# Summing the first block of rows of a graph attention layer densely instead of over gathered edges

## The chip, the core and the metric

The kernel runs on one NeuronCore of a Trainium2 chip. Five engines work side by side, each through its own queue in order: TensorE (PE in the profile; its weight loads are shown as PEld), VectorE (DVE), ScalarE (ACT), GpSimd (POOL) and SyncE (SP, which here only issues transfers). The metric is the device time of one launch in microseconds (us); lower is better. One core means one core's span and one granted TensorE clock.

## The reference, cut to what matters

The program is four graph layers in a row over the same 3327 nodes with 512 features, each followed by a residual sum and a layer norm. The adjacency matrix has 26,715 edges in all and its density falls with the row number: the first 128 rows hold 4,829 of them (row 0 has 223 neighbours, row 10 has 62). Only layer 0, a graph attention layer with 8 heads of 64 features, is touched:

```python
Wh = jnp.einsum('nd,hdo->hno', x, W)            # 8 heads x 3327 x 64
f1 = jnp.einsum('hno,ho->hn', Wh, a1)
f2 = jnp.einsum('hno,ho->hn', Wh, a2)
e = jax.nn.leaky_relu(f1[:, :, None] + f2[:, None, :], negative_slope=0.2)
e = jnp.where(adj[None, :, :] > 0, e, NEG_INF)
h_prime = jnp.einsum('hnm,hmo->hno', jax.nn.softmax(e, axis=-1), Wh)
x = _layernorm(x + elu(h_prime as 3327 x 512))
# layer 1: mean over neighbours, two weights, relu; layer 2: mean over the first 64 neighbours;
# layer 3: attention again, 4 heads of 128
```

## The kernel before

The rows are 26 blocks of 128 (the last has 127). For each block the kernel makes an edge list from the adjacency matrix, and each layer then gathers the rows of its neighbours by that list, 128 edges (a chunk) per indirect transfer, and sums them with a selection matrix on TensorE. The lists of block 1 to 25 have 19 down to 5 chunks, 201 together. Block 0 is too dense for one list: three lists (`HEAVY`, L527) of 14 chunks, 42 together.

**Edge lists** (`structure`, L848). Python generators order the work. A block's two halves of the adjacency matrix are loaded into two tiles `ab` (one buffer each, 832 KB, L857), turned into a 0/1 mask by ScalarE (L864), multiplied by a code of the column (L874) and searched on VectorE for the eight largest values of each segment (L892). For block 0 each segment is searched three times, with the found values replaced between (L894). L904 and L906 sort the candidates into slots, and L943 to L957 spread the slots over the 128 partitions as `idx` and `dst`. Each `yield` in `structure` is one turn; a regular block takes five to seven turns, block 0 takes 30 (three lists of ten) and one more at its end. The order of the blocks is 1, 2, 3, 0, 4, ... (`FIRST`, L543). Layers 2 and 3 and the second half of layer 1 treat block 0 by its dense mask `row0` and need no list of it; layer 0 alone uses its three lists.

**Prologue.** While lists are made, `projection` (L1338) loads each block of `x`, transposes it, multiplies it by the weights of layer 0 (L1017) and stores rows of 528 numbers (8 heads of 64 features and two scores) to the table `t0_d`. After each projection three turns of `structure` are taken. `finish` (L1034) closes the table; the first gather can then start.

**Layer 0.** The loop at L1480 takes one group of up to four chunks per step and advances every unfinished generator by one stage (`Stages.step`), and takes one turn of `structure` (two on each eighth step). A group (`Gat.group`, L1188) gathers its chunks on POOL's queue (L981), computes their scores (L1206 to L1231) and weights (L1238), and adds 2 matmuls per chunk into two PSUM tiles `acc` (L1247). The pool of these has four buffers, so that two blocks' sums can be open. After a block's last group `layer0_end` (L1432) divides by the softmax sum (L1260 to L1264), makes elu, residual and layer norm (L1273 to L840), multiplies by the weights of layer 1 (L780) and stores rows to `t1_d`; block 0 to 9 also store a product with a second weight to `z1_d`.

A scheduler decides the order of instructions on each engine up to the end of layer 0 from this program order and its own estimates. From layer 1 on the program order is kept as written. Layer 1 gathers from `t1_d` and so starts when all 26 blocks are stored; four independent products (`self_part`) are placed ahead of it.

Layer 3 already sums its block 0 densely (`first_block`, L1147): for each of the 26 blocks of rows it makes a weight matrix of 128 by 128 per head with VectorE (L1170, L1172), a mask with ScalarE (L1165), and one matmul per head (L1175), with rows that are still in PSUM. This stage is not touched by the change, and its rows serve as prices.

Of the kernel before, what the change touches and what calls it, by code (L numbers as in the profile page):

```python
# [8 lines left out]
F32 = mybir.dt.float32  # L9
# [520 lines left out]
HEAVY = ((0, 9, 1760, 120, 9, 3), (9, 18, 1792, 120, 9, 3), (18, 27, 1792, 120, 9, 3))  # L530
# [12 lines left out]
FIRST = 3  # L543
# [5 lines left out]
class EdgeList:  # L549


    def __init__(self, pool, name, cuts, room, K, rounds, at):
        self.cuts, self.room, self.K, self.rounds, self.at = cuts, room, K, rounds, at
        L = self.L = -(-room // P)
        self.idx = pool.tile([P, L], U32, name=f"idx{name}")
        self.dst = pool.tile([P, L], BF16, name=f"dst{name}")
        self.nmid = pool.tile([P, 1], F32, name=f"nmid{name}")
# [18 lines left out]
class Ring:  # L576
# [20 lines left out]
    def done(self):  # L597

        self.live.pop(0)

# [22 lines left out]
def sparse_path(ctx, tc, flag_i, x, adj, l0_w, l0_a1, l0_a2, l1_w_self, l1_b_self, l1_w_nb, l1_b_nb,  # L623
# [35 lines left out]
    for b in range(NB):  # L659
        parts = HEAVY if b == 0 else ((0, SEGMENTS[b], CAPS[b], SLOTS[b], SEGMENTS[b], 1),)  # L660
        total = parts[-1][1]
        lists.append([])
        for q, (s0, s1, room, K, n, rounds) in enumerate(parts):
            cuts = [int(NP * ((s0 + (s1 - s0) * s / n) / total) ** 2) // 2 * 2 for s in range(n + 1)]
            cuts = [c for i, c in enumerate(cuts) if i in (0, n) or c >= 8 * rounds]
            lists[b].append(EdgeList(keep, f"{b}_{q}", cuts, room, K, rounds, sum(map(len, lists)) - 0))
# [176 lines left out]
    def structure(big, mid, ps, m0):  # L843
# [26 lines left out]
        for k, b in enumerate(order):  # L870
            ab = fetch(order[k + 1]) if k + 1 < NB else None
            val = big.tile([P, NP], U16, name="val")
            for s in range(2):
                nc.vector.tensor_mul(val[:, s * HW:(s + 1) * HW], ms[s], code[:, s * HW:(s + 1) * HW])  # L874
            many = len(lists[b]) > 1
            if many:
                nc.vector.tensor_add(deg[:, b:b + 1], half[:, 0, b:b + 1], half[:, 1, b:b + 1])
                lone = mid.tile([P, 1], F32, name="lone")
                nc.vector.tensor_scalar(lone, deg[:, b:b + 1], 0.0, None, ALU.is_equal)
            for q, l in enumerate(lists[b]):  # L880
                L, K, cuts, rounds, a = l.L, l.K, l.cuts, l.rounds, l.at
                dg = dgs[:, a:a + 1]
                start = starts[:, a:a + 1]
                if not many:
                    nc.vector.tensor_scalar(dg, half[:, 0, b:b + 1], half[:, 1, b:b + 1], 1.0, ALU.add, ALU.max)
                n = (len(cuts) - 1) * rounds
                cand = mid.tile([P, n, 8], F32, name="cand")
                for s in range(len(cuts) - 1):
                    seg = val[:, cuts[s]:cuts[s + 1]]
                    for r in range(rounds):  # L890
                        top = cand[:, s * rounds + r, :]
                        nc.vector.max(out=top, in_=seg)  # L892
                        if r + 1 < rounds:
                            nc.vector.match_replace(out=seg, in_to_replace=top, in_values=seg, imm_value=0.0)  # L894
                    if s == (len(cuts) - 1) // 2:
                        if q == 0 and ab is not None:
# [12 lines left out]
                if not many:  # L909
                    nc.vector.tensor_scalar(slots[:, 0:1], slots[:, 0:1], 1.0, None, ALU.max)  # L910
                elif q == 0:
                    nc.vector.tensor_tensor(slots[:, 0:1], slots[:, 0:1], lone, ALU.max)
                    nc.vector.tensor_tensor(dg, lone, cnt[:, a:a + 1], ALU.max)
                else:
                    nc.vector.tensor_copy(dg, cnt[:, a:a + 1])
# [86 lines left out]
    class Gat:  # L1002
        def __init__(self, name, table, H, OUT, w, k):
# [5 lines left out]
            self.opened, self.free = False, True  # L1009

# [22 lines left out]
        def finish(self, pool, ps):  # L1033
# [5 lines left out]
            n = 4 * H if self.k else 2 * H  # L1039
# [834 lines left out]
```

## Time and profile before

| | us |
|---|---|
| median of 3 runs (lowest, highest) | 1853.08 (1841.69, 1855.64) |
| the profiled execution, its own time | 1863.64 |
| its span | 1861.8 |
| prologue: start to the first group's work | 0 to 224 |
| layer 0 up to the end of block 18 | 224 to 655 |
| of this from block 3's norm to block 0's norm | 349 to 424 |
| last seven blocks of layer 0 up to the first products for layer 1 | 655 to 740 |
| layers 1, 2 and 3 | 740 to 1862 |

The stage boundaries are read from the start of ScalarE's layer norm step (L840) of each block in the trace. The profile gives, per engine, the time that its instructions cover. A matmul's record lasts longer than its place in the stream: the starts of neighbouring records, not their lengths, tell what it costs TensorE. An fp32 matmul stands as two records. A window's answer gives the busy time of each engine in that stretch, the number of instructions, the granted TensorE clock and the mean busy share of the DMA engines. The granted clock of the whole execution was 0.919.

### The profile page before, as it was taken

What the parts mean: (1) busy time and instruction counts of PE and PEld (TensorE: products, weight loads), DVE (VectorE), ACT (ScalarE), POOL (GpSimd) and SP (SyncE); (2) the same over time, 40 slices, a digit from 0 to 9 for tenths busy, and PEclk for the clock granted to TensorE, in tenths of its full rate; (3) what the DMA queues carried; (4) which work ended last, traced back from release to release, by engine and by line L of the source; (5) the groups of instructions that cost most, each with busy time, mean ns of one, the idle gap of its engine ahead of it and who ended that gap; (6) DMA issues with size and microseconds to landing.
All of it is one profiled execution on the core that took longest, in us unless ns stands there. A gap on an engine that the chain in (4) does not pass through costs nothing.

```text
span 1861.8 us, 24835 instructions
## 1 busy us (share of the span) xinstructions
PE 1556.7 (84%) x7669; PEld 1020.7 (55%) x7707; DVE 1232.2 (66%) x3224; ACT 788.8 (42%) x2525; POOL 893.4 (48%) x981
## 2 busy tenths in 40 slices
PE   5898758988989998899999987568997946778774
PEld 4665545665656665455555543135665725666553
DVE  8999857878877863255566765365654525676776
ACT  6557835555666664122111111014443423454564
POOL 1000166556555531655556632666665246666650
PEclk9899879989999999799999989788998977888988
DMA  9524776777675632999999983877887346666661
GB/s 305 206 77 134 263 248 188 261 236 214 235 221 158 214 122 84 385 352 332 320 350 345 376 294 109 274 250 237 282 280 249 130 119 170 187 189 191 199 175 36
DMA packets 126658, 418.72 MB, mean 225 GB/s; under 512 B 23539, under 2 KB 25075, under 8 KB 126516
## 3 DMA queue, kind: packets, MB, share of 16 engines
q0 software_dynamic: 81472, 304.52, 51.4%
q1 hardware_dynamic: 45044, 112.52, 17.1%
q8 instruction: 63, 1.03, 0.2%
q14 instruction: 79, 0.65, 0.1%
HBM read 368.66 MB, written 48.30 MB: 224 GB/s over the span
## 4 chain that ended last, share of the span: by engine, by line
PE 60%; DVE 18%; issue 6%; another core or an unknown queue 6%; ACT 4%; DMA 4%; POOL 1%; SPq 0%; DVEq 0%; ACTq 0%; POOLq 0%
PE po L780 18%; PE acc L1247 18%; PE acc L1555 10%; PE po L1017 5%; DVE cand L892 2%; PE pt L765 2%; PE pg L1218 2%; DMA gm<-t_d,idx 2%; DVE gt L1238 1%; DVE cand L906 1%; PE acc L1175 1%; DVE sl L904 1%; DVE val L874 1%; DVE st L785 1%
## 5 line engine op out<-in xcount | busy, mean ns | idle before, releaser
L981 POOL DMA_INDIRECT gl<-t_d,idx x334 | 331.8, 993 | 273.4 <-issue 73.3
L981 POOL DMA_INDIRECT gt<-t_d,idx x243 | 242.3, 997 | 384.2 <-DVE sl L910 211.2
L1247 PE MATMUL acc<-gt,sel 128*128 128x264 f32 (+2 forms) x972 | 248.7, 403 | 1.3 <-issue 0.7
L1247 PE MATMUL acc<-gl,sel 128*128 128x260 f32 (+3 forms) x684 | 191.6, 430 | 48.1 <-issue 40.1
L981 POOL DMA_INDIRECT gm<-t_d,idx x159 | 159.1, 1001 | 115.3 <-PE acc L1555 55.9
L1247 PEld LDWEIGHTS acc<-gt,sel 128*128 128x128 f32 (+2 forms) x972 | 184.2, 196 | 51.9 <-issue 23.4
L780 PE MATMUL po<-wn,xt 128*128 128x512 f32 x416 | 201.2, 628 | 12.5 <-ACT vc L946 6.1
L1247 PEld LDWEIGHTS acc<-gl,sel 128*128 128x128 f32 (+3 forms) x684 | 139.1, 211 | 82.1 <-issue 51.2
L1238 DVE TENSOR_TENSOR gt<-gt,pg 128x1536 f32<-128x1536 f32 (+3 forms) x75 | 140.6, 1874 | 9.3 <-issue 4.7
L780 PEld LDWEIGHTS po<-wn,xt 128*128 128x128 f32 x416 | 80.8, 200 | 101.6 <-issue 84.4
L1555 PE MATMUL acc<-gm,selr 128*128 128x512 f32 (+2 forms) x360 | 118.6, 460 | 9.0 <-DMA gm<-t_d,idx 5.8
L892 DVE MAX8 cand<-val 128x8 f32<-128x832 uint16 (+38 forms) x259 | 125.1, 522 | 0.0
L1017 PE MATMUL po<-w,xt 128*128 128x262 f32 x416 | 104.0, 406 | 21.4 <-ACT xt L772 21.3
L768 ACT COPY xt<-pt 128x512 f32<-128x512 f32 x81 | 47.4, 591 | 149.2 <-PE pt L765 85.8
L1017 PE MATMUL po<-gt,xt 128*128 128x268 f32 x416 | 108.0, 406 | 2.6 <-ACT xt L772 1.3
L765 PE MATMUL pt<-s_ident,xres 128*128 128x128 f32 x500 | 77.5, 281 | 37.4 <-DMA xres<-in_x_dram 16.5
L1218 PEld LDWEIGHTS <-ds 128*128 128x128 bf16 x1332 | 55.6, 99 | 91.8 <-issue 43.2
L1206 ACT ACTIVATE far<-place,nmid 128x384 int16<-128x384 int16 (+3 forms) x137 | 86.9, 638 | 43.5 <-DVE ds L1210 36.2
L1017 PEld LDWEIGHTS po<-w,xt 128*128 128x128 f32 x416 | 82.2, 201 | 41.6 <-ACT xt L772 24.1
L780 PE MATMUL po<-wx,xt 128*128 128x512 f32 x208 | 97.5, 616 | 4.3 <-ACT vc L946 4.3
L1238 DVE TENSOR_TENSOR gl<-gl,pg 128x1536 f32<-128x1536 f32 (+3 forms) x53 | 98.2, 1852 | 2.2 <-issue 1.2
L1230 ACT ACTIVATE pg<-sc 128x24 f32<-128x24 f32 (+5 forms) x137 | 26.0, 190 | 164.3 <-DVE sc L1229 105.6
(309 smaller groups left out, 3042.4 us busy)
## 6 DMA issues: line engine op xcount, KB each, us to landing
ab<-in_adj_dram SPq DMA_DIRECT2D x25, 832.0 KB
ab<-in_adj_dram SPq DMA_DIRECT2D x25, 831.5 KB
t_d<-t SPq DMA_DIRECT2D x25, 512.0 KB
gm<-t_d POOLq DMA_DIRECT2D x20, 512.0 KB
t_d<-t SPq DMA_DIRECT2D x25, 384.0 KB
t_d<-tg SPq DMA_DIRECT2D x25, 264.0 KB
t_d<-tg SPq DMA_DIRECT2D x25, 260.0 KB
xres<-in_x_dram SPq DMA_DIRECT2D x25, 256.0 KB
```

The source lines that it names most:

```text
L765: nc.tensor.transpose(pt[:, c, :], src[:, c * P:(c + 1) * P], ident)
L768: nc.scalar.copy(xt, pt)
L780: nc.tensor.matmul(po, xt[:, c, :], w[:, c], start=c == 0, stop=c == DC - 1)
L892: nc.vector.max(out=top, in_=seg)
L981: nc.gpsimd.indirect_dma_start(out=t[:m, c, :], out_offset=None, in_=table[:, :], in_offset=bass.IndirectOffsetOnAxis(ap=l.idx[:m, c0 + c: ...
L1017: nc.tensor.matmul(pw[s], xt[:, c, :], self.w[:, c, s, :], start=c == 0, stop=c == DC - 1)
L1206: nc.scalar.activation(far[:, :g * P], place[:, c0 * P:(c0 + g) * P], AF.Abs, bias=l.nmid, scale=2.0)
L1218: nc.tensor.matmul(pe[:, c], ds[:, c * P:(c + 1) * P], self.own[:, k, :, b], start=k == 0, stop=k == 2)
L1230: nc.scalar.activation(w[:, :g], sc[:, :g, 0], AF.Exp)
L1238: nc.vector.tensor_mul(Gc[:, :, :OUT], Gc[:, :, :OUT], w[:, :g].rearrange("p c (h o) -> p (c h) o", o=1).to_broadcast([P, g * H, OUT]))
L1247: nc.tensor.matmul(accs[b][s], S[:m, c, :], G[:m, c, s * hh * M:(s + 1) * hh * M], start=at + c == 0, stop=at + c == chunks_of[b] - 1)
L1555: nc.tensor.matmul(accs[b], chosen, parts[:, k * D:(k + 1) * D], start=at + c + k == 0, stop=k == top and at + c == n - 1)
```

## The change

Block 0 gets no edge list; its turn in `structure` only makes its mask and its degree, and the order of the blocks becomes 1, 0, 2, 3, ... Its sum in layer 0 is made from all 26 blocks of table rows j: load the 128 rows of `t0_d` (270 KB, on SP's queue, three buffers), take three exponentials of scores and the mask `row0` on ScalarE, scale each head's 64 features by its exponential on ScalarE (8 activations), build the 128 x 8 x 128 weights on VectorE (a maximum and a product), and add 8 matmuls (65 weight columns, 128 moving columns) into a pair of PSUM tiles. These steps are fed two after each group of the last seven blocks. When j = 25 is done the row of the mean is added for rows without neighbours, and the sum is turned by 8 transposes to the form that `layer0_end` reads. While the dense pair is open, the other blocks use one pair of PSUM tiles (`turn` stays 0), and a group whose pair is taken waits (`held`). The scratch tiles come from the room of the two transposed weights and a new pool `l0d`. `structure` now takes two turns on every step.

```diff
-HEAVY = ((0, 9, 1760, 120, 9, 3), (9, 18, 1792, 120, 9, 3), (18, 27, 1792, 120, 9, 3))
-FIRST = 3
+FIRST = 1
+DENSE = 7
...
         for k, b in enumerate(order):
             ab = fetch(order[k + 1]) if k + 1 < NB else None
+            if b == 0:
+                nc.vector.tensor_add(deg[:, 0:1], half[:, 0, 0:1], half[:, 1, 0:1])
+                ms = masks(order[k + 1], ab)
+                yield k
+                continue
...
+            while self.held[self.turn] if at == 0 else b not in accs:
+                yield
             if at == 0:
-                accs[b] = [pacc.tile([P, 512], F32, name="acc")[:, :hh * M].rearrange("p (h m) -> p h m", h=hh)
-                           for s in range(2)]
+                accs[b] = self.sums(pacc, self.turn)
+                self.turn ^= not self.pinned
...
+        def open_dense(self, pool, ps, pacc, *spaces):
...
+            for s in range(2):
+                pf = ps.tile([P, hh * P], F32, name="pf", tag="po")
+                nc.tensor.matmul(pf, ones, self.wt[0][:, s * hh:(s + 1) * hh], start=True, stop=True)
+                nc.scalar.activation(self.up[:, s * hh:(s + 1) * hh], pf.rearrange("p (h i) -> p h i", i=P),
+                                     AF.Exp, scale=1.0 - GAT_ALPHA)
+                yield
+            while self.held[1]:
+                yield
...
+            for s in range(2):
+                nc.tensor.matmul(self.acc[s][:OUT + 1], self.nil, self.up[0:1, s * hh:(s + 1) * hh],
+                                 start=True, stop=False)
+        def dense(self, j, pool, ps, pacc, done):
...
+            for p0, p1 in rows_of(j):
+                nc.sync.dma_start(gd[p0:p1], self.table[2 + j * P + p0:2 + j * P + p1, :])
+            mask = pool.tile([P, P], F32, name="mk", bufs=2)
+            nc.scalar.activation(mask, row0[:, j, :], AF.Identity)
+            yield
...
+            nc.vector.tensor_sub(fs[:m, 0], g[:m, :, OUT], self.cmax[:m])
+            nc.scalar.activation(fs[:m, 1], fs[:m, 0], AF.Exp, scale=GAT_ALPHA - 1.0)
+            nc.scalar.activation(g[:m, :, OUT], fs[:m, 0], AF.Exp)
+            yield
+            for h in range(H):
+                nc.scalar.activation(g[:m, h, :OUT], g[:m, h, :OUT], AF.Identity, scale=g[:m, h, OUT:OUT + 1])
+            nc.vector.tensor_tensor(wt[:m], self.up[:m], fs[:m, 1, :, None].to_broadcast([m, H, P]), ALU.max)
+            nc.vector.tensor_mul(wt[:m], wt[:m], mask[:m, None, :].to_broadcast([m, H, P]))
+            yield
...
+            for h in range(H):
+                nc.tensor.matmul(out(h), g[:m, h, :OUT + 1], wt[:m, h, :], start=False, stop=False)
...
+            for h in range(H):
+                nc.tensor.matmul(out(h), g[:, h, :OUT + 1], lone, start=False, stop=False)
+            for s in range(2):
+                nc.tensor.matmul(self.acc[s][:OUT + 1], self.nil, self.up[0:1, s * hh:(s + 1) * hh],
+                                 start=False, stop=True)
...
+                nc.scalar.copy(turned[:, s], self.acc[s][:OUT + 1])
...
+                nc.tensor.transpose(acc[h // hh][:, h % hh, :OUT + 1],
+                                    turned[:, h // hh, h % hh * P:(h % hh + 1) * P], ident[:OUT + 1, :OUT + 1])
+            self.pinned = False
+            done(0, acc)
...
-             pool_in(lay, "l0pa", 4, space=PSUM), pool_in(lay, "l0p2", 2, space=PSUM))
+             pool_in(lay, "l0pa", 2, space=PSUM), pool_in(lay, "l0p2", 2, space=PSUM))
...
+            for item in groups(pools[0], (b,)):
+                yield item
+                for _ in range(2):
+                    if left and n >= len(blocks) - DENSE:
+                        yield left.pop(0)
...
-        more(2 if k % 8 == 0 else 1)
+        more(2)
```

With the two tags `acc0` and `acc1` the pool of two buffers still holds four PSUM tiles. In `layer0_end` block 0 skips one pause before its second product, and layer 3's final check counts found edges for blocks 1 to 25 only.

## The prediction, made before the changed kernel ran

> **What bounds the kernel now.** I read the page first, then the engines by stage, then single rows of the stages that the change touches.
>
> ```profile
> PE 1556.7 (84%) x7669; PEld 1020.7 (55%) x7707; DVE 1232.2 (66%) x3224; ACT 788.8 (42%) x2525; POOL 893.4 (48%) x981
> ...
> PE 60%; DVE 18%; issue 6%; another core or an unknown queue 6%; ACT 4%; DMA 4%; POOL 1%; SPq 0%; DVEq 0%; ACTq 0%; POOLq 0%
> ```
>
> TensorE carries most of the chain that ended last, VectorE the next part. The windows say where which of them does (busy us of PE, PEld, DVE, ACT, POOL; clock; DMA share; GB/s):
>
> ```profile
> 0.00:224.00 224.00, 183.18 (x1059) 131.10 (x1059) 209.10 (x789) 148.12 (x513) 11.67 (x29) 0.95 0.57 191
> 224.00:655.00 431.00, 367.02 (x2265) 258.08 (x2266) 327.98 (x825) 241.39 (x697) 248.69 (x272) 0.93 0.70 222
> 655.00:740.00 85.00, 77.18 (x369) 47.76 (x369) 44.98 (x107) 45.20 (x127) 15.18 (x25) 0.96 0.28 94
> ```
>
> The prologue is VectorE's: 209.1 of 224 us (93%), PE 82%. Layer 0 is TensorE's: 85% in its long part, 91% in its last seven blocks, where VectorE and ScalarE stand at 53%. From 740 us on nothing is edited; I cost it at 0.
>
> The rows for prices, by shape (count | busy us, mean ns), first of the prologue, then of layer 0, then of layer 3's own dense block:
>
> ```profile
> L874 DVE TENSOR_TENSOR val<-m,code 128x1664 uint16<-128x1664 bf16 x22 | 22.3, 1014 | 0.1
> L904 DVE MAX8 sl<-cand 128x8 f32<-128x216 f32 x30 | 11.6, 385 | 0.9
> L906 DVE MATCH_REPLACE8 cand<-sl,cand 128x216 f32<-128x216 f32 x28 | 10.3, 367 | 0.0
> L952 DVE TENSOR_TENSOR eq<-slot,off 128x480 int16<-128x480 int16 x10 | 6.4, 644 | 0.0
> ```
>
> ```profile
> L1238 DVE TENSOR_TENSOR gt<-gt,pg 128x1024 f32<-128x1024 f32 x7 | 8.4, 1205 | 0.1
> L1264 ACT ACTIVATE h<-acc,rden 128x64 f32<-128x64 f32 x208 | 47.9, 334 | 3.6 <-DVE rden L1261 3.5
> ```
>
> ```profile
> L1175 PE MATMUL acc<-g,wt 128*128 128x129 f32 x200 | 27.1, 278 | 3.8 <-DVE wt L1172 3.8
> ...
> L1165 ACT ACTIVATE mk<-row 128x128 f32<-128x128 fp8e4 x26 | 9.3, 360 | 0.0
> ```
>
> Two entries of the chain in order of time give TensorE's stream price for gathered edges, two lines of its timeline (start, us) that for the dense sum:
>
> ```profile
> 283.19 3.62 PE acc L1247 x16
> ```
>
> ```profile
> 1335.35 1.06 PE L1175 MATMUL acc<-g,wt 128*128 128x129 f32 x8
> 1336.24 0.60 PE L765 MATMUL pt<-s_ident,xres 128*128 128x128 f32 x4
> ```
>
> **Prologue.** Block 0's lists leave VectorE. There go 2 products of 1.01 us, 81 segment searches at 0.28 (the mean segment has 123 columns; the row of 124 columns has 281 ns), 54 replacements at about 0.28, 30 maxima at 0.385 and 15 at 0.334, 28 replacements at 0.367 and 14 at 0.317, 42 loads ahead of these at 0.088, and 12 unpacking steps at 1.99 (0.644 + 0.640 + 0.397 + 0.31 for two small ones): 2 + 23 + 15 + 17 + 15 + 4 + 24, some 100 us with small change, 95 after overlap of neighbours. The prologue still takes three turns per projection, so the 30 turns go to other blocks, 5 each: 6 more blocks. One costs 2.0 (products) + 4.3 (six searches, 0.25 to 1.21) + 1.2 + 1.1 + 1.0 = 9.6 us; 58 us come back. VectorE then has 209 - 95 + 58 = 172 us. ScalarE loses 19 us (12 pairs of L938 and L946 at 1.3, and smaller ones) and gains 6 x 6.0 (two masks at 1.6 + 0.22, the rest 2.4): 165. TensorE's 183 stay. Six more blocks of adjacency (10 MB) are loaded into single buffers: between 164 and 219.5 us the masks came every 9.25 us, so that 17 blocks need about 157 us and the first 14: 171. VectorE is no longer alone; TensorE's 183, of which it showed 82%, is the next. The prologue ends between 183 (all of the 41 us) and 224 (a new pace-maker as slow as VectorE; a loss would need masks every 12 us and I exclude it). I take 200, the middle: **-24 us**.
>
> **Layer 0 up to block 18.** Block 0's 42 chunks leave. Four chunks cost PE 3.62 us for 16 records, and 0.43 + 0.35 for 12 score and 4 transposing matmuls (the weight loads of L1218 and L1224 at 226 us): 4.40, 1.10 a chunk, 46.2 us. At the 88% that PE showed from 349 to 424 this frees 53 us. VectorE also loses 12 groups at 2.9 us and the 58 us of lists made earlier: 328 - 35 - 58 = 235 in some 370 us, 64% where it was 76%. I count 12 us for fewer waits of PE (bounds 0 and 22, which would be the 91% of the last blocks): **-65**. `more(2)` brings the remaining lists forward into the first third of this stage, where VectorE may again pace it; this is why I take no more. POOL loses 42 gathers at 1.25 us from start to start; it is waiting for ring room anyway: 0.
>
> **The dense stretch**, laid over the last seven blocks. PE: 8 records of L1175 took 0.89 us to the next start, 0.111 each (from above, 27.1/200 = 0.135). A block j has 16: 1.78, 26 of them 46.3 us (56 by the upper price). Opening and closing: 2 + 4 fp32 matmuls of 512 columns (12 records at 0.43, as L780), 16 records for the lone rows, 8 transposes at 0.11: 7.8. So PE has 77 + 54 = 131 us: **what TensorE gave up in front it takes on again here; its sum is nearly unchanged.** VectorE: 45 + 26 x (2 x 1.205 + 0.24) = 114. ScalarE: 45 + 26 x (0.36 + 0.40 + 8 x 0.23) + 2.4 = 115, with 0.23 = 47.9/208; by the records' own length of 0.334 it would be 137. The loads are 26 x 270 KB into a stretch that moved 94 GB/s. They stand on SP's in-order queue with the stores of `t1_d`, which wait for VectorE, and each waits for the matmuls three blocks back; I cost them at 0 because three blocks of work (over 15 us) cover them; without that cover nine rounds of three would wait one landing each (a store of that size stands with 5.46 us in the chain at 202.8 us): 49 us.
>
> Three engines at 131, 114 and 115 no longer hide each other as 77, 45 and 45 did. With PE at the 91% of before the stretch takes 144 us, at the 75% that I put as the lower end (PE 73% and 82% are the poorest stages of its own, 224 to 260 us aside) 175. I take 87%, near the long stage: 151, that is **+66** for 85 before (bounds +59 and +90). Behind the last j stand the row of the mean, two copies of 65 x 512, the transposes and block 0's own end. Block 25 had such an end before; the extra part is about 4 us of serial steps, of which other ends hide nothing for certain: **+3**. Block 0's second product without its pause (8 records, 3.45 us) lies beside the four early products: 0.
>
> [...] ScalarE's row above reads PSUM and takes 0.23 us in the stream. [...]
>
> **Sum.** -24 - 65 + 66 + 3 = -20 us. Against the profiled execution's own 1863.6 that is 1843; the median of the runs is 10.6 lower, and from it I get **1833**. About 1% is what a measurement of this kernel can tell from no change.
>
> **The rivals.** *A: the work is better spread and more is won.* For it: TensorE reached 92% (212 of 231 us) from 424 to 655 with VectorE at 81%, so the scheduler can pack two full engines. Prologue -38, front -72, stretch +60, close +2: -48, 1805. Against it: three engines are full here.
>
> *B: it cancels.* The front is won, the prologue only half (adjacency loads pace it), the stretch runs at 80% (164, +79): -12 - 58 + 79 + 5 = +14 at worst, and about +2 with a prologue of -24: 1855. For it: the matmuls of a dense block wait for eight activations one by one on an engine that is nearly full.
>
> *C: slower, by the one pair of sum tiles.* While the dense pair is open each of the seven blocks hands its `acc` pair to the next. Before, two pairs alternated. At 683.2 us a block's last matmul ended and the last of its eight L1264 at 688.5: 5.3 us. With two dense blocks' scalings ahead of it in ScalarE's queue (2 x 8 x 0.23) that is 9 us, 7 times 63, in which PE can only do the dense matmuls at hand (1.8 to 3.6 us) and a product (3.45). My 87% holds 7 us of this; all of it uncovered gives +56 more: 1889. It makes the kernel slower by over 1% when a handover leaves TensorE idle for 6.5 us more than I have counted, on the mean.
>
> *D: it does not do what it says.* The new bound on the scores could send the program into its general path, many times slower; the largest 0.8 x (f1 + f2) of these inputs is 15 and the limit 60. I give it 1%, with C.
>
> **Chances.** The forecast (-10 to -35) 0.40, A 0.20, B 0.22, C and D 0.18. Two thirds of the forecast's case lie beyond 1% (1834.5): faster 0.27 + 0.20 = 0.47; same 0.13 + 0.22 = 0.35; slower 0.18. The range leaves out the lowest part of A and most of C: 1795 to 1877. The likeliest case alone is 1818 to 1843.
>
> **What would show it.** The first gather on POOL at 195 to 205 us (now 221); VectorE's busy time before it near 172. The norms of the blocks 1 to 18 done by about 565 us. In the dense stretch records of L1324 about 0.11 us apart, scalings of L1315 0.23 to 0.28 apart, VectorE's two products at 1.2. If C holds, TensorE's first `acc` matmul of a block waits for ScalarE's division. If the loads are late, ScalarE's second exponential waits for a transfer. What would make me wrong most: the share of TensorE in the stretch, on which 30 us hang, and a prologue that is paced by loads.

## The result, and the profile after

The changed kernel takes **1848.51 us** (median, 1835.21 to 1853.63) against 1852.22 us for the kernel before (1841.69 to 1859.94). The ratio is 0.9973, with a 95% interval from 0.9957 to 0.9990: about 5 us faster, a quarter of the 20 us forecast, and within the 1% that the prediction called no change. One execution in the experiments below, of e3, took 8539 us; nothing here explains it, and it stands outside the comparison. The profiled executions span 1850.1 us (clock 0.918) and 1861.8 (0.919).

The page of the changed kernel, the engines' busy time and the shares of the chain that ended last:

```profile
PE 1564.0 (85%) x7729; PEld 1030.3 (56%) x7729; DVE 1192.6 (64%) x2887; ACT 821.9 (44%) x2728; POOL 856.0 (46%) x936
...
PE 46%; DVE 6%; issue 4%; another core or an unknown queue 4%; ACT 3%; DMA 2%; POOL 1%; DVEq 0%; ACTq 0%; POOLq 0%
```

VectorE lost 40 us of work, ScalarE gained 33, and TensorE's sum rose by 7 (1556.7 before). The shares of the chain sum to about two thirds, because in this trace it can be followed back only to about 629 us, into the end of layer 0, so the windows have to speak. The same three as before (busy us of PE, PEld, DVE, ACT, POOL; clock; DMA share; GB/s):

```profile
0.00:224.00 224.00, 181.34 (x1101) 131.90 (x1101) 183.22 (x586) 164.51 (x549) 18.06 (x37) 0.94 0.76 251
224.00:655.00 431.00, 375.05 (x2220) 264.88 (x2221) 310.74 (x705) 254.67 (x816) 217.31 (x236) 0.93 0.62 187
655.00:740.00 85.00, 79.15 (x405) 52.56 (x404) 49.15 (x95) 49.87 (x178) 9.32 (x13) 0.94 0.23 72
```

In the prologue VectorE fell from 209.1 to 183.2 us, but these windows are cut at the times of the kernel before. More is seen when they are cut where the work itself changes stage: at the first gather, at the norms of the blocks 3 and 18, and at the last norm of layer 0. The kernel before, cut so:

```profile
0.00:221.10 221.10, 182.12 (x1043) 130.32 (x1044) 206.20 (x781) 145.22 (x508) 9.17 (x28) 0.95 0.57 191
221.10:349.60 128.50, 89.81 (x634) 67.66 (x633) 89.87 (x215) 62.30 (x167) 82.46 (x86) 0.84 0.75 230
349.60:656.20 306.60, 278.72 (x1650) 191.22 (x1650) 242.02 (x622) 182.83 (x540) 169.74 (x190) 0.96 0.68 219
656.20:723.60 67.40, 62.99 (x319) 40.83 (x320) 40.23 (x99) 40.06 (x118) 13.83 (x23) 0.95 0.27 91
```

The changed kernel, cut at the same four events:

```profile
0.00:212.30 212.30, 178.27 (x1053) 129.46 (x1053) 175.69 (x559) 157.00 (x530) 9.10 (x28) 0.97 0.75 248
212.30:375.70 163.40, 111.83 (x746) 81.89 (x746) 124.01 (x335) 84.06 (x233) 94.33 (x97) 0.81 0.72 224
375.70:591.00 215.30, 207.84 (x1139) 140.96 (x1140) 142.93 (x314) 129.60 (x414) 108.67 (x126) 0.98 0.59 175
591.00:720.10 129.10, 118.80 (x732) 87.80 (x729) 97.43 (x175) 93.13 (x358) 29.68 (x32) 0.96 0.36 107
```

The second column is the stage's length, the third TensorE's busy time; the difference is its idle time.

| stage | before | after | difference | forecast | TensorE idle before, after |
|---|---|---|---|---|---|
| prologue, to the first gather | 221.1 | 212.3 | -8.8 | -24 | 39.0, 34.0 |
| blocks 1 to 3 | 128.5 | 163.4 | +34.9 | | 38.7, 51.6 |
| on to the end of block 18 (block 0 in it before) | 306.6 | 215.3 | -91.3 | | 27.9, 7.5 |
| front of layer 0, the last two together | 435.1 | 378.7 | -56.4 | -65 | 66.6, 59.0 |
| the last seven blocks and the closing | 67.4 | 129.1 | +61.7 | +69 | 4.4, 10.3 |
| layer 0 | 723.6 | 720.1 | -3.5 | -20 | 110.0, 103.4 |

TensorE is busy for 613.6 us of layer 0 before and 616.7 after. On the whole the change carries its work from the front to the end, so that all of the gain had to come out of its 110 us of idle time, and 6.6 came. Behind layer 0 nothing is edited; single profiles of that rest scatter by some 10 us (1138 and 1130 here), so the times decide on the whole and the traces on the stages.

The prices held. The groups of the dense sum by shape (count | busy us, mean ns | idle before), and three entries of the engines' timelines (start, us):

```profile
L1324 PE MATMUL acct<-raw,gd 128*65 128x128 f32 x400 | 48.6, 273 | 3.1 <-ACT xres L844 1.6 <-ACT gd L1315 1.0 <-issue 0.5
L1315 ACT ACTIVATE gd<-gd 128x64 f32<-128x64 f32 x184 | 47.8, 344 | 0.3
...
L1317 DVE TENSOR_TENSOR raw<-raw,mk 128x1024 f32<-128x1024 f32 x25 | 30.5, 1219 | 0.2
```

```profile
657.82 1.74 ACT L1365 ACTIVATE h<-acc,rden 128x64 f32<-128x64 f32 x8
...
660.12 2.04 ACT L1315 ACTIVATE gd<-gd 128x64 f32<-128x64 f32 x8
...
661.56 1.91 PE L1324 MATMUL acct<-raw,gd 128*65 128x128 f32 x16
```

A dense j costs TensorE 1.91 us (1.78 forecast), VectorE 2 x 1.22 (2 x 1.205), and a scaling 0.255 us.

### The profile page after: what moved, and what is told of

It reads as the page before. It is cut to its first block, busy times and chain, and to the rows that moved or that the text cites. A ratio compares the mean times of both kernels' runs of the same rounds, so it can differ in the third digit from the quotient of the medians.

```text
span 1850.1 us, 24775 instructions
## 1 busy us (share of the span) xinstructions
PE 1564.0 (85%) x7729; PEld 1030.3 (56%) x7729; DVE 1192.6 (64%) x2887; ACT 821.9 (44%) x2728; POOL 856.0 (46%) x936
## 3 DMA queue, kind: packets, MB, share of 16 engines
q0 software_dynamic: 78128, 293.23, 50.1%
## 4 chain that ended last, share of the span: by engine, by line
PE 46%; DVE 6%; issue 4%; another core or an unknown queue 4%; ACT 3%; DMA 2%; POOL 1%; DVEq 0%; ACTq 0%; POOLq 0%
PE po L784 14%; PE acc L1681 11%; PE acc L1249 10%; PE po L1010 5%; PE pt L769 2%; PE acc L1175 1%; PE pg L1218 1%; PE acc L1757 1%; PE acct L1324 1%; DVE st L789 1%; DMA gm<-t_d 1%; POOL gm L973 1%; ACT h L1365 1%; DMA gm<-t_d,idx 1%
## 5 line engine op out<-in xcount | busy, mean ns | idle before, releaser
L973 POOL DMA_INDIRECT gt<-t_d,idx x201 | 200.8, 999 | 371.1 <-DVE off L942 202.5
L1249 PE MATMUL acc<-gt,sel 128*128 128x264 f32 (+3 forms) x804 | 212.5, 412 | 1.5 <-issue 1.4
L784 PE MATMUL po<-wn,xt 128*128 128x512 f32 x416 | 195.9, 614 | 10.1 <-ACT xt L772 4.9
L1249 PEld LDWEIGHTS acc<-gt,sel 128*128 128x128 f32 (+3 forms) x804 | 154.3, 201 | 47.0 <-issue 17.7
L1238 DVE TENSOR_TENSOR gt<-gt,pg 128x1536 f32<-128x1536 f32 (+3 forms) x63 | 116.5, 1849 | 16.8 <-ACT sel L1233 11.3
L769 PE MATMUL pt<-s_ident,xres 128*128 128x128 f32 x500 | 78.3, 284 | 33.6 <-DMA xres<-in_x_dram 17.1
L892 DVE MAX8 cand<-val 128x8 f32<-128x464 uint16 (+32 forms) x184 | 106.1, 619 | 0.0
L1218 PEld LDWEIGHTS <-ds 128*128 128x128 bf16 x1206 | 51.3, 99 | 92.5 <-issue 59.4
L1681 PEld LDWEIGHTS acc<-gm,selr 128*128 128x128 f32 (+2 forms) x360 | 67.5, 201 | 47.2 <-issue 21.6
L784 PE MATMUL po<-wl,xt 128*128 128x512 f32 x208 | 93.1, 593 | 0.0
```

Source lines behind the costliest of these rows:

```text
L769: nc.tensor.transpose(pt[:, c, :], src[:, c * P:(c + 1) * P], ident)
L784: nc.tensor.matmul(po, xt[:, c, :], w[:, c], start=c == 0, stop=c == DC - 1)
L892: nc.vector.max(out=cand[:, s, :], in_=val[:, cuts[s]:cuts[s + 1]])
L973: nc.gpsimd.indirect_dma_start(out=t[:m, c, :], out_offset=None, in_=table[:, :], in_offset=bass.IndirectOffsetOnAxis(ap=l.idx[:m, c0 + c: ...
L1218: nc.tensor.matmul(pe[:, c], ds[:, c * P:(c + 1) * P], self.own[:, k, :, b], start=k == 0, stop=k == 2)
L1238: nc.vector.tensor_mul(Gc[:, :, :OUT], Gc[:, :, :OUT], w[:, :g].rearrange("p c (h o) -> p (c h) o", o=1).to_broadcast([P, g * H, OUT]))
```

## The experiments

Edits are against the changed kernel unless said otherwise. Differences "to the changed kernel" divide the two ratios to the kernel before and are given in us of 1852 (of 1704 on the faster chip); where the changed kernel ran beside them, its median is used. Their 95% intervals are about 6 us to either side. Four chips took part in the experiments. On three of them the kernel before takes 1848 to 1862 us; on the fourth it takes 1704. The first three are called the slower chips; e9, e10, e11 and e16 to e18 ran on the faster one.

### What paces the prologue: e1, e2, e8, e14

The fused weights are products of layer 1's weight matrices, which the kernel makes once, in the prologue. e1 leaves out TensorE's part of them:

```
-                    rt = transposed(xp, ps, raw)
                     yield
-                    po = times(ps, rt, wc[:, s * DC:(s + 1) * DC, :])
-                    nc.scalar.copy(o[:, i, :], po)
+                    nc.scalar.copy(o[:, i, :], raw)
```

> The changed kernel without TensorE's part of layer 1's fused weights (32 transposes and 32 products of 512 columns in the prologue are left out, the raw weights are copied in their place; everything else, the lists and the adjacency loads too, stays). The part left out is about 8 x (0.60 + 4 x 0.45) = 19 us of TensorE. Theory T (since VectorE has fewer lists, TensorE paces the prologue: 120.1 of 125 us busy from 75 to 200 us): the first gather moves from 212.3 to 193 to 199 us, and the kernel is 13 to 19 us faster than the changed one. Rival L (adjacency loads and list work pace it, DMA share 0.76 as against 0.57 before): the first gather stays within 4 us of 212 and so does the time.

First gather at 198.5 us (212.3); ratio 0.9894 (0.9862 to 0.9925), which is 15 us faster than the changed kernel. Both lie where T put them, and L, by which nothing moves, is out. But TensorE's busy time to the first gather fell by 30 us, not by the 19 of the estimate (each of its 32 products stands as two records of about 0.43 us, and the estimate counted one):

```profile
0.00:198.50 198.50, 148.35 (x957) 113.31 (x957) 174.38 (x565) 154.99 (x529) 9.09 (x28) 0.95 0.81 270
```

So 14 of 30 us came back, and the other 16 became idle time (50.1 us from 34.0) with VectorE at 88%. TensorE's work is thus the limit for part of the way; what holds the rest was not separated. The order counts too: e14, below, keeps more of TensorE's work in the prologue than e1 and ends it 6 us sooner.

e2 lightens the list work in the prologue instead (`more(3)` becomes `more(2)`):

> The changed kernel with two turns of the list work per projection in the prologue, not three: about 11 instead of 17 blocks' adjacency is loaded and listed there. Rival L (loads and lists pace the prologue, one block every 9.5 us): the first gather falls by 25 us or more, to 187 us or less. Theory T (TensorE paces it): only what TensorE still idles can go, 9.3 us between 17 and 75 us, where VectorE is 96% busy, and 5 between 75 and 200: the first gather at 202 to 210 us. Six more lists then lie in the first third of layer 0, where VectorE already has 86%: the time of the whole is 0 to 15 us longer than the changed kernel's.

First gather at 204.3 us, 8 earlier and not 25; ratio 1.0035 (1.0012 to 1.0058), 11 us slower than the changed kernel. This fits T and not L: in this prologue VectorE is busy for only 136.5 of 204.3 us, and TensorE for 172.0, so that 6 of the 8 us are the lists' own matmuls that TensorE no longer has there (178.3 before the edit):

```profile
0.00:204.30 204.30, 171.96 (x963) 125.18 (x964) 136.48 (x422) 135.43 (x476) 9.09 (x28) 0.97 0.66 220
```

The middle of the prologue, first in the kernel before, then in the changed kernel, shows why VectorE's relief was worth so little:

```profile
75.00:200.00 125.00, 114.58 (x649) 81.44 (x648) 120.22 (x483) 82.49 (x303) 0.00 (x0) 0.97 0.42 142
```

```profile
75.00:200.00 125.00, 120.09 (x727) 87.21 (x726) 100.36 (x336) 102.28 (x364) 0.00 (x0) 1.00 0.71 240
```

VectorE gave up 20 us and TensorE could take only 5.5: it was already at 92% and is now at 96%. Half of the 34.0 us for which it idles in the prologue cannot be reached from VectorE, as the waits say (us in total, times, longest; first of the kernel before, then of the changed kernel):

```profile
PE pt L765 <- DMA xres<-in_x_dram: 16.5, 1, 16.5
```

```profile
PE pt L769 <- DMA xres<-in_x_dram: 17.1, 1, 17.1
```

Those 17.1 us at the very start are the load of the first rows. With 178.3 us of work behind them the prologue of the changed kernel cannot end before 195 us. The other 16.9 us up to 212.3 are short waits for VectorE and ScalarE, none over 3 us.

e8 moves TensorE's work out of the prologue, behind the last table rows:

```
-            if t == 4:
+            if t == 18:
                 fused.add(fused_weights())
...
         work.drain(more)
-        fused.drain(more)
         g0.finish(xp, ps)
+        fused.drain(more)
```

> The changed kernel with layer 1's fused weights begun with projection 18 instead of 4, and what is left of them put behind the last projection and the score maxima: some 13 us of TensorE's work moves from ahead of the last table rows to behind them, into 200 to 260 us, where TensorE is busy for 25.9 of 60 us. Theory T (TensorE paces the prologue and then waits for the table): the first gather falls by 8 to 14 us from 212.3, and the kernel is 6 to 14 us faster than the changed one. Rival L (loads and lists pace the prologue): the first gather and the time stay within 4 us.

First gather at 190.1 us, ratio 0.9855 (0.9830 to 0.9880): 22 us faster than the changed kernel, more than T gave. e14 repeats it beside the changed kernel (e12), since a stall of the first groups in the changed kernel could have had a part in that:

> The changed kernel with the fused weights late, beside the changed kernel on the same chip: theory T (TensorE paces the prologue): 15 to 25 us faster; if the 22 us came from a stall of the first groups that this order avoids by chance: 6 to 14 us where the changed kernel does not show that stall.

1824.99 us against 1844.82: 20 us faster. First the two stages of the changed kernel on that chip (e12), then those of e14, to the first gather and on to the end of block 3:

```profile
0.00:210.20 210.20, 176.81 (x1053) 129.12 (x1053) 175.71 (x557) 156.42 (x530) 9.05 (x27) 0.97 0.76 251
210.20:369.20 159.00, 109.58 (x746) 81.04 (x746) 123.98 (x337) 83.67 (x232) 94.71 (x97) 0.83 0.73 230
```

```profile
0.00:192.20 192.20, 157.48 (x983) 119.46 (x984) 170.65 (x544) 154.38 (x522) 12.47 (x27) 0.97 0.83 277
192.20:347.80 155.60, 123.43 (x778) 84.65 (x778) 131.34 (x383) 86.44 (x241) 88.40 (x91) 0.89 0.71 225
```

TensorE's 19 us leave the first stage, which gets 18 us shorter, and 14 appear in the second, whose length does not grow: its idle time falls from 49 to 32 us. Work put behind the last projection is free here, because TensorE idles there for 49 us in any case. The stall can have only a small part in it: e12 shows one (ScalarE stands still from 221.2 to 235.7 us, TensorE waits for 13.8 us in one piece) and e14 none (behind the load of the first rows no wait of TensorE is over 3.3 us), but from the one to the other the stage in which it lies gets 3 us shorter, the one ahead of it 18. On the faster chip, where the changed kernel shows no such stall, the late weights with the slow lists (e11) are worth about 20 us as well.

### The pace of the lists: e3, e4, e13, e11, e15

e3 and e13 undo one part of the change:

```
-        more(2)
+        more(2 if k % 8 == 0 else 1)
```

> The changed kernel with the lists in layer 0's main part made at the pace of before (one turn per group, two with every eighth), not two turns per group. Theory P (the hastened lists are paid for: blocks 1 to 3 took 162.5 us from the first gather, 127.7 before, with VectorE 99.4 of 115 us busy): block 3 ends at 340 to 355 us instead of 374.8, not all of it is given back later, and the kernel is 8 to 20 us faster than the changed one. Rival M (VectorE's lists are only moved, TensorE's sum decides): block 3 ends earlier, but block 18 ends at 590 within 5 us, and the time is within 4 us of the changed kernel's.

> The changed kernel with the lists of layer 0's main part at the pace of before, beside the changed kernel. The profile had layer 0's end 6 us earlier, the times said 6 us later. Theory P (hastening costs): 5 to 12 us faster than the changed kernel. Rival M (the list work is only moved): within 4 us.

e3: ratio 1.0007 (0.9982 to 1.0031). e13: 1850.99 us against 1844.82 beside it. Both are 6 us slower than the changed kernel, each at the edge of its interval. P is wrong, and M only nearly right: in e13 block 3 ends 138 us after the first gather (159 in e12), but the next part takes 242 us (213), and block 18 is 8.5 us later, counted from the first gather. In the profile of e3 layer 0 was 6 us shorter; its times say otherwise and stand.

e4 makes the same edit alone in the kernel before:

> The kernel before with one edit alone: two turns of the list work with every group of layer 0. Theory P: the hastening costs by itself, 8 to 20 us more than the kernel before. Rival M: within 4 us of it.

Ratio 1.0032 (1.0005 to 1.0059), 6 us slower than the kernel before. So the hastened lists cost some 6 us in the one kernel and are worth some 6 in the other. The blocks 1 to 3 pay in both (156 us in e4, 129 before), and what is given back differs; that it depends on what VectorE has to do later is likely and not tested.

e11 and e15 put both edits together, late weights and slow lists:

> The changed kernel with the fused weights late (the edit that gave 22 us) and the lists of layer 0's main part at the pace of before (one turn per group). Between 240 and 350 us TensorE was busy for 92.3 of 110 us and VectorE for 95.9; from 350 to 568 VectorE had 64%. If the lists spread over that time lengthen nothing (theory P): 5 to 12 us faster than with the fused weights late alone. If they are only moved (M): within 4 us of it.

> Fused weights late and lists at the pace of before, beside the three others. Theory P: 5 to 12 us faster than with the fused weights late alone. Theory M: within 4 us of it.

e15: 1820.95 us, ratio 0.9869 (0.9825 to 0.9913), against 1824.99 for the late weights alone: 4 us less, which with six times of each does not tell M from the lower end of P. On the slower chips e14 and e15 are 1.2% and 1.3% faster than the kernel before, and 20 and 24 us faster than the changed one. e11, on the faster chip, has a ratio of 0.9996 (0.9981 to 1.0011) to the kernel before; it stands again below.

### What the dense sum costs, and what sets it: e5, e6, e7, e9, e10, e18

e5 returns from `dense` after three empty steps for all j but the last.

> The changed kernel without the sums over the blocks 0 to 24 of rows: their loads, masks, exponentials, scalings, VectorE products and matmuls are left out (25 of 26 j), the opening, the last j and the closing stay. It gives the price of the dense sum in its place. Forecast: TensorE 25 x 1.78 = 44.5 us at a share of 87 to 92%: 48 to 52 us faster than the changed kernel, with layer 0's end at 667 to 672 us instead of 719.3. If VectorE, ScalarE or the handovers paced the stretch (rivals B and C), more goes: 60 us or more.

Ratio 0.9764 (0.9727 to 0.9801): 39 us faster than the changed kernel, layer 0's end at 682.1. That is less than the forecast, and less than the 48 us that 25 j cost TensorE by their own rows (25 x 1.91): up to the end of layer 0 its busy time fell by 43 us and its idle time rose by 5. The stretch itself:

```profile
583.20:682.10 98.90, 86.81 (x398) 54.10 (x396) 51.48 (x115) 47.00 (x145) 21.74 (x33) 0.91 0.27 90
```

It is 30 us shorter than in the changed kernel; the other 8 us lie ahead of the end of block 18, where the first dense blocks are. It is still 31.5 us longer than the 67.4 of before. In these lie the opening, the last j, the closing, block 0's own end, and 34 more records of gathered sums still to do when block 18 ends (144 in e5, 110 before).

e6 takes half of the matmuls away (`for h in range(0, H, 2)`), e7 the scalings:

```
-            for h in range(H):
-                nc.scalar.activation(g[:m, h, :OUT], g[:m, h, :OUT], AF.Identity, scale=g[:m, h, OUT:OUT + 1])
+            nc.scalar.activation(g[:m, :, :OUT], g[:m, :, :OUT], AF.Identity, scale=0.0)
```

> The changed kernel with half of the dense matmuls left out (4 of 8 heads in each j); all loads, scalings and VectorE products stay. TensorE loses 208 records at 0.111 = 23 us. Theory T (TensorE alone paces the dense stretch, 119.8 of 130 us busy): 18 to 25 us faster than the changed kernel. Rival (the chain through ScalarE's scalings and VectorE's products, or the one pair of sum tiles, paces it): 0 to 8 us faster.

> The changed kernel with the 208 scalings on ScalarE left out (eight activations of 64 columns in each j replaced by one of 512 columns by a constant); all else stays. ScalarE loses some 26 x (8 x 0.33 - 0.6) = 53 us of records in the stretch. Theory T (TensorE paces it): within 4 us of the changed kernel. Rival (ScalarE's one-by-one scalings pace the dense blocks): 15 to 40 us faster.

e6: ratio 0.9933 (0.9909 to 0.9958), 7 us (with an interval of 2 to 13) faster than the changed kernel for 23 us of TensorE: theory T, by which 18 to 25 go, falls here. e7: 0.9972 (0.9949 to 0.9995), no difference: ScalarE is not it either. The next theory (K) was that VectorE and TensorE fill the stretch together. e9 makes VectorE's two products for 4 heads only, e10 and e18 take half of the matmuls away as well (the last four heads, where e6 left out every second one):

```
-            nc.vector.tensor_tensor(wt[:m], self.up[:m], fs[:m, 1, :, None].to_broadcast([m, H, P]), ALU.max)
-            nc.vector.tensor_mul(wt[:m], wt[:m], mask[:m, None, :].to_broadcast([m, H, P]))
+            nc.vector.tensor_tensor(wt[:m, :hh], self.up[:m, :hh], fs[:m, 1, :hh, None].to_broadcast([m, hh, P]), ALU.max)
+            nc.vector.tensor_mul(wt[:m, :hh], wt[:m, :hh], mask[:m, None, :].to_broadcast([m, hh, P]))
```

> The changed kernel with VectorE's two products of a dense j made for 4 heads instead of 8 (the other 4 heads' matmuls take the same weights); all matmuls, scalings and loads stay. VectorE loses 26 x 2 x 0.6 = 31 us in the dense stretch. Theory K (the products of VectorE and the matmuls of TensorE both fill the stretch, so that taking one away alone leaves the other, as half of the matmuls did with 2.5 us at layer 0's end): within 6 us of the changed kernel, layer 0's end at 714 to 721 us. Rival V (VectorE alone paces it): 20 to 30 us faster, layer 0's end at 690 to 700.

> The changed kernel with half of the dense matmuls and half of VectorE's products left out (4 of 8 heads), the scalings on ScalarE, loads and the number of steps staying. Theory K: with both lightened the stretch gets shorter by about half of what the whole dense sum costs (38 us at layer 0's end): 15 to 25 us, layer 0's end at 695 to 705 us. Rival O (neither engine's work but the order of the steps, one dense j after the other with waits between the engines, sets the stretch): 0 to 8 us, layer 0's end at 712 to 720.

> The changed kernel with half of the dense matmuls and half of VectorE's dense products left out (4 of 8 heads), beside the changed kernel. Theory K (both engines fill the dense stretch): 14 to 22 us faster; half of the matmuls alone gave 7. Rival O (the order of the steps sets the stretch): within 9 us.

All three ran on the faster chip, where the changed kernel takes 1726.48 us (e17); the times of layer 0's end expected of e9 and e10 were meant for a slower one and cannot be compared. e9 and e10 ran at another time than e17, so their ratios to the kernel before count: e9 1.0108 (1.0080 to 1.0136) against 1.0116, 1 us faster, which is no difference; e10 1.0000 (0.9986 to 1.0014), 20 us faster. e18, beside e17, takes 1705.58, 21 us faster. The profiles agree. From the first gather to the end of layer 0 there are 470 us in e17, 469 in e9, 452 in e10 and 454 in e18. On the slower chips the same stretch takes 508 and 502 us in the changed kernel (first measurement and e12) and 506 in e6. So half of VectorE's share gives next to nothing, half of TensorE's 7 us by the times and less by the profiles, and both together some 20: theory K. One gap is left: half of the matmuls alone was not run on the faster chip. The windows from the end of block 18 to the end of layer 0, of e6, e9 and e18 in this order:

```profile
594.00:717.60 123.60, 101.59 (x513) 66.03 (x511) 92.20 (x168) 88.75 (x339) 21.11 (x27) 0.90 0.31 95
```

```profile
548.30:677.80 129.50, 120.56 (x745) 89.63 (x743) 78.65 (x176) 93.88 (x364) 22.86 (x33) 0.96 0.34 106
```

```profile
544.70:663.00 118.30, 105.02 (x577) 72.39 (x575) 77.04 (x176) 93.44 (x366) 24.03 (x33) 0.94 0.39 120
```

In e6 TensorE's 17 us less turned into 12 us more of idle time (22 of 123.6, from 10.3 of 129.1). In e9 VectorE's 19 us less left the stretch as long as it was (129.5). In e18 both are lighter, and it is 10.5 us shorter than in e17; 6 us more of its gain lie ahead of block 18's end, where the first dense blocks are. Another 6.5 us lie before the first gather, where nothing differs: e17's first gather, at 215.9 us, is late beside 209 to 211 in e9, e10 and e18.

### The same two kernels on two kinds of chip: e12, e16, e17

> The changed kernel itself, beside the three others of this call on the same chip, since the chips differ (the kernel before takes 1850 and 1862 us on two and 1704 on a third, where gathers land faster). If the change is worth the same everywhere: a ratio of 0.996 to 0.999 to the kernel before. If it loses where gathers are fast (TensorE then waits less for block 0's gathered edges, which the change replaces): 1.000 to 1.010 on the fast chip.

> The kernel before, profiled on the same chip as the next two. Stage by stage (first gather, end of block 3, end of block 18, end of layer 0) it should repeat 221, 350, 656 and 724 us on a chip of the slower kind. On the faster chip (1704 us) its gathers land sooner: block 3 at 310 to 330 us, the end of layer 0 at 670 to 690.

> The changed kernel beside the kernel before. On a chip of the slower kind: ratio 0.996 to 0.999, layer 0's end 3 to 10 us earlier. On the faster chip: 1.000 to 1.012, since there TensorE waits less for gathered edges, and the dense sum of the same TensorE time replaces work that no longer waits.

e12, on a slower chip: 0.9979 (0.9958 to 1.0000), 3 us faster than the kernel before, close to the first measurement. e17, on the faster chip: 1726.48 us, ratio **1.0116** (1.0098 to 1.0134): 20 us slower. The stages there, first of the kernel before (e16), then of the changed kernel:

```profile
0.00:221.00 221.00, 181.76 (x1043) 130.19 (x1044) 206.31 (x781) 145.28 (x508) 9.13 (x27) 0.96 0.57 191
221.00:328.20 107.20, 85.64 (x633) 65.49 (x633) 88.28 (x215) 62.35 (x166) 83.25 (x86) 0.89 0.85 272
328.20:597.20 269.00, 265.04 (x1650) 187.81 (x1650) 240.99 (x622) 184.32 (x539) 171.12 (x190) 0.99 0.78 250
597.20:664.00 66.80, 62.68 (x319) 40.91 (x319) 40.36 (x99) 40.09 (x118) 13.73 (x23) 0.95 0.28 93
```

```profile
0.00:215.90 215.90, 179.83 (x1053) 130.85 (x1053) 175.94 (x560) 157.06 (x530) 9.10 (x28) 0.95 0.74 245
215.90:350.00 134.10, 107.00 (x746) 79.89 (x746) 123.13 (x335) 83.28 (x232) 97.99 (x97) 0.87 0.82 272
350.00:557.30 207.30, 203.59 (x1134) 139.19 (x1135) 142.90 (x314) 129.48 (x415) 107.07 (x126) 0.99 0.61 183
557.30:686.10 128.80, 119.29 (x736) 88.38 (x734) 97.47 (x175) 93.13 (x358) 29.73 (x32) 0.96 0.36 107
```

The stretch (+62) is what it was on the slower chip, and the prologue (-5) nearly so. The front is not: before, it takes 376 us here, not 435. Of these 59 us, 41 are idle time of TensorE (25.5 us here, 66.6 there) and 18 its busy time, at a higher granted clock (0.89 and 0.99 here, 0.84 and 0.96 there). Taking out block 0's gathered edges then saves 35 us, not 56: TensorE's work in the front falls by 40 us and its idle time rises by 5. The sum is +22 at layer 0's end. The late weights and slow lists are worth about 20 us here too (e11, 0.9996 against 1.0116) and bring the changed kernel back to the kernel before. The late weights in the kernel before itself were not tried.

## Why the prediction was right and wrong

**Right in mechanism, and on the slower chips in sign.** TensorE has the most work in layer 0 and takes on again at the end what it gives up in front: 613.6 us and 616.7, as the forecast said. The stretch was priced at +66 and the closing at +3; they took +62 together. The loads of the dense blocks, costed at 0, hold VectorE for 2.3 us in the stretch.

**Wrong: the prologue, -24 forecast, -9 found.** The step that failed is "I take 200, the middle" between 183 and 224. The lower end, 183, was TensorE's own busy time and left out the load ahead of its first matmul (16.5 us in the kernel before, 17.1 in the changed one). With it the floor was 200 already, for a TensorE that never waits again. What the runs showed: 178.3 us of TensorE's work, 17.1 of this load and 16.9 of short waits, 212.3 in all. VectorE's 172 came out nearly right (175.7); what took its place was mainly the next engine, TensorE at 96% in the middle. e14 shows it best: 19 us of TensorE's work put elsewhere make the prologue 18 us shorter. By e1 this holds for part of the way only. Rival B had the prologue only half won, but for adjacency loads; e2 lightened these and gained 8 us, of which TensorE's own lighter work is 6.

**Mis-sized: the front, -65 forecast, -56 found.** TensorE's busy time fell by 49 us there (46.2 forecast). Of the idle time, 19 us were to go (7 as the share of the 46, 12 for fewer waits), and 7.5 went. The part behind block 3 gave more than that (27.9 to 7.5 us); the blocks 1 to 3 took it back (38.7 to 51.6), where the hastened lists load VectorE (76% against 70%). The prediction named them ("VectorE may again pace it") and put no number to them; e4 shows that on their own they cost some 6 us, e3 and e13 that here they are worth some 6 on the whole.

**Near in sum, wrong in its working: the stretch.** The forecast took TensorE's 77 + 54 = 131 us at a share of 87%. In the bounds of the stages measured here that is 63 + 54 = 117 us; 118.8 were found, at a share of 92%, near the 91% that the forecast took for its bound. But e6 shows that TensorE is not alone the measure: without half of the dense matmuls only about 7 us go. TensorE and VectorE share the stretch, and only a cut in both shortens it by most of the work taken out. The forecast reckoned by TensorE's share alone, so that its sum came near is in part luck.

**The rivals.** A has the stretch with its closing exactly (+62) and fails in the prologue (-38) and the front (-72). C fails: TensorE idles for 10.3 of 129 us in the stretch, and its weight loads for `acc` wait for ScalarE's division for 0.6 us in all. B comes nearest in the outcome, with prologue and front right in size, but its stretch (+84 with the closing) is 22 us too long, and the adjacency loads were not its cause. D did not happen.

**The price of a scaling.** The forecast took 0.23 us for each of the 208 scalings, from ScalarE's row of L1264, which reads PSUM; the new scalings read SBUF. In the timeline above eight of L1365 (from PSUM) take 1.74 us, eight of L1315 (from SBUF) 2.04: 0.037 us more each. By e7, where all the scalings together cost nothing that can be measured (ratio 0.9972 without them, 0.9973 with them), it does not matter to the time.

**Missed altogether:** that the size of the front, and with it the sign, hangs on how long TensorE idles there, which differs from chip to chip (66.6 and 25.5 us in the kernel before). All numbers of the prediction came from one profile of a slower chip. Why the chips differ stays open; see the last section.

## What to carry to other kernels

When a change takes work off the engine that seems to pace a stage, the floor is the next engine's busy time plus the waits that the first engine never caused, the first load above all; and it is a floor, not the lower end of an even range. When it moves work on the bounding engine from one place to another, only that engine's idle time in the two places can be won, so write down busy and idle by stage, cut at events of the program, before costing anything else. And where the gain has to come out of idle time, measure on more than one chip: the same edit was 0.2 to 0.3% faster on two slower chips and 1.2% slower on the faster one.

## What the runs showed of the hardware that was not expected

**Chips differ by 8 to 9% on this kernel.** 1848 to 1862 us on three chips, 1704 on a fourth. Layers 1 to 3 of the kernel before take 1138 us on a slower chip and 1037 on the faster one at a granted clock of 0.91 and 0.94. The front of layer 0 moves about the same bytes in less time there (219 to 230 GB/s and 250 to 272), which does not say what is cause and what effect. The expectations of e12 and e16 put it down to gathers that land sooner. The list of transfers cannot tell: it has the gathers of layer 0 without a landing time on the slower chip, and with one, in us, on the faster (kernel before on both):

```profile
gt<-t_d,idx POOLq DMA_INDIRECT x243
```

```profile
gt<-t_d,idx POOLq DMA_INDIRECT x243, 4.7
```

The single packets are in the trace on both chips, though, among them 16 of four bytes for each gather. Counted off in order, the last of a gather's 16 ends 3.6 us (median) after the issue in the changed kernel on the slower chip and 3.7 on the faster one (e17), and 3.7 and 4.1 us in the kernel before. Where the list of e17 gives a landing (75 gathers), it lies 0.4 us behind this count. So the traces do not bear out that gathers land sooner on the faster chip.

**A stall without a releaser.** In the changed kernel on a slower chip TensorE, VectorE and ScalarE all stand still for 15 to 20 us shortly after the first gather, while POOL goes on issuing gathers. First TensorE's wait, then a window inside the stall:

```profile
PE pg L1218 <- issue: 19.4, 2, 19.2
```

```profile
223.40:238.40 15.00, 0.00 (x0) 0.00 (x0) 0.00 (x0) 0.01 (x1) 11.34 (x13) 0.50 0.73 209
```

The kernel before has such a stall too (VectorE from 239.3 to 252.9 us). On the faster chip the first sum starts 16 us after the first gather in both kernels, on the slower one 35 us after it in the changed kernel and 18 in the kernel before. It would be natural to take these stalls for waits for slow gathers, but by the count of packets the first 24 gathers landed within 5 us each, those of the stall among them. What the engines wait for the trace does not name. The granted clock stands at 0.50 from 213 to 250 us there, around the stall; in e17 it does so from 213 to 237 us without a stall of this kind.
